# Two transformer blocks on one core: the last pair of maxima in its own slot, outputs in their own list, three things placed elsewhere

## The chip, the core and the metric

The kernel runs on one core of a Trainium2 chip. The core has a matrix engine (TensorE, PE in the profile, with its weight loads as PEld), a vector engine (DVE), a scalar engine (ACT), GpSimd (POOL), and SyncE (SP), which issues most of the DMAs. Each engine works through its own instruction stream in order and waits on semaphores for the others. PE writes only to PSUM, eight banks of 128 x 512 f32, from where DVE or ACT must take the result before the bank is used again. The metric is the device time of one execution in microseconds.

## What is computed

Two layers, each of them self-attention, cross-attention over a context, and a gated feed-forward, on x of 4 x 512 x 320 with a context of 4 x 1601 x 192, 20 heads of 16, all f32:

```python
h1 = _ln(x, n1_g, n1_b)
x = _attn(h1, h1, q1, k1, v1, o1_w, o1_b, heads) + x
h2 = _ln(x, n2_g, n2_b)
x = _attn(h2, context, q2, k2, v2, o2_w, o2_b, heads) + x
h3 = _ln(x, n3_g, n3_b)
a, g = jnp.split(h3 @ ff_w1 + ff_b1, 2, axis=-1)
return a * jax.nn.gelu(g, approximate=False) @ ff_w2 + ff_b2 + x
```

`_attn` is softmax attention: scores of queries and keys, less their row maximum, exponentials, times the values, divided by the sum of the exponentials, and an output projection.

## The kernel before

**Units.** The work of attention is cut into units: one batch row and one group of four heads. A layer has 20 self units (4 rows x 5 groups, 512 keys, 4 chunks of 128 keys), 20 cross units (1601 keys, 13 chunks) and 4 feed-forward units. Numbered over the whole program, layer 0 has self units 0 to 19, cross units 20 to 39 and feed-forward units 40 to 43; layer 1 the same from 44 on.

**Two passes over the scores.** A unit's scores are computed twice. First with queries on partitions, in tiles of 128 queries, only to take the row maxima: PE line L1088 (and L1113 for the 65 last keys of cross units) into tile `sps`, DVE line L1099 (L1123) takes the maximum. `max_end` (L1162 on) then negates and splits the maxima, transposes them on DVE (L1175) and sends them with four small DMAs (L1183) into a tile of rows, `nrows`. The second pass has keys on partitions, in `main`: three accumulating matmuls for each chunk and head (L1336, tile `st`), the third of them adding the negated maxima; ACT takes the exponential (L1346); PE multiplies by the values (L1362, tile `av`), ACT copies that out (L1376 for a unit's first chunk, into the unit's tile `o`, of which there are two; L1381 for the others) and POOL adds it up (L1382).

**Rounds and slots.** The array works with 32 rows per head, so matmuls of four heads run beside one another. A step of `main` handles one chunk: two half-steps, called rounds by the clock of the schedule. In each of them two heads' second-pass scores (three passes of the array) share the array with one *pair* of maximum tiles on the other two row groups (two passes). A self unit has 8 pairs in two lists of 4, a cross unit 26 pairs in two lists of 13; `u.pairs[0]` is served at even rounds and `u.pairs[1]` at odd ones. A unit has as many rounds as pairs: 8 or 26. `giver(u)` (L1643) returns `give(h)`, which hands out the regular pair of round h, always for a unit that comes later: the next unit while it has pairs in the list of that parity, otherwise the one after. It also decides on *extra rounds* (`round_of` on two pairs, one of each list, alone on PE): when the pairs that are due outnumber the rounds left, and when the next unit has any pair left at the last round before its `max_end`, that is round 3 of a self unit and round 21 of a cross unit (the test `rest == 1`).

**The planner.** All other work is put into lists, `chains`, each entry with a cost, a due round and two conditions. At every step `steps` takes the head with the earliest due round, as long as credit allows; entries of cost zero are DMAs and the like. Within a list the order is fixed. Three things here belong to it:

- `add_finish` (L1194) puts what follows a unit's last chunk into the list "divide": first `turn`, which sends the tile `o` to DRAM (`oway`, L1203), two rounds or more after the last chunk. For the last group of a batch row follow the reciprocal of the sums, its way to DRAM and back, and the division of the gathered outputs by parts (`read`, `load`, `divide`, `end`), with waits of several rounds between them.
- `add_turned` (L751) turns batch row b's context: seven pieces, each transposed on DVE (L767) into one of two tiles by turns (`room["turned"]`, in the profile a part of `stages`), and saved to DRAM by a DMA (L775, `ctxT<-stages`). For row 0 of layer 0 this lies under self units 5 to 8; the pieces have due rounds `gap` apart, the last one `gap` before round 70. The transpose of piece i+2 overwrites the tile that the save of piece i reads. `add_context` loads the saved context for the keys (L789).
- `expect` is the planner's model of when PE, ACT and DVE will be done; `bank` (L410) gives out the PSUM bank that this model expects to be free first. It only chooses banks.

**The start.** Before the first unit, the projections and maxima of unit 0 are done by hand, with DMAs on both SP and ACT (`start["on"]`). `at_once(units[2])` issues unit 2's moves: keys on SP, and queries (`q<-halves`, L888) on ACT.

Of the kernel before, what the change touches and what calls it, by code (L numbers as in the profile page):

```python
# [78 lines left out]
def kernel(ctx: ExitStack, tc: tile.TileContext, x, context, ws, out):  # L79
# [313 lines left out]

    chains = {n: deque() for n in ("divide", "project", "norm", "scale", "context", "early", "proj", "values")}
    clock = {"round": 0, "credit": 0.0, "lights": 0, "tiles": None, "ff": False, "cross": False}
    ALIKE = ("project", "early", "proj", "values")
    LIGHT = 0.01
# [42 lines left out]
    def add(chain, cost, f, due, ready=yes, soon=yes):  # L442
        chains[chain].append((cost if isinstance(cost, tuple) else (cost,), due, ready, soon, f))
# [396 lines left out]
    def add_proj(u):  # L840
# [35 lines left out]
        def move(of, pairs, may, gap=0):  # L876

            def f():
                pending[of] -= 1
                if of == "k":  # L880
                    room["sent"] = clock["round"]
                u.moving[of] = clock["round"]
                for to, src in pairs():
                    queue = nc.sync
                    if start["on"]:
                        queue = (nc.sync, nc.scalar)[room["first"] % 2]
                        room["first"] += 1
                    queue.dma_start(out=to.bitcast(F32), in_=src)  # L888
                u.open -= 1
                if not u.open:  # L890
                    u.when = -9 if start["on"] else clock["round"]

            pending[of] += 1
            u.moves[of].append((f, may, gap))
            u.moving[of] = clock["round"]
            if (u.i, of, u) not in movers:
                movers.append((u.i, of, u))
# [266 lines left out]
    def max_end(u):  # L1164

        top, high, low = (u.nm[:, :, i, :] for i in range(3))
        nc.vector.tensor_reduce(
            high.bitcast(F32R), top.rearrange("p j (t o) -> p j t o", o=1), AX.X, ALU.max, negate=True
        )
        nc.vector.tensor_reduce(  # L1170
            low, u.nm[:, :, 0:2, :].rearrange("p j e t -> p j t e"), AX.X, ALU.add, negate=True
        )
        turned = two.tile([P, SLOT], F32, tag="turned", name="turned")

        nc.vector.transpose(turned.rearrange("p (j c) -> p j c", j=HG), u.nm[:, :, 1:3, :].rearrange("p j e t -> p j (e t)"))  # L1175
        busy("dve", 0.6)
        slots = u.rows.bitcast(F32).rearrange("(g s) n -> s g n", s=DH)[0].rearrange("g (t r) -> g t r", t=NQ)

        def rows():
            for i in range(P // SLOT):  # L1180
                part = slice(i * SLOT, (i + 1) * SLOT)
                queue = nc.scalar if start["on"] and i % 2 else nc.sync
                queue.dma_start(out=slots[:, :, part], in_=turned[part, :])  # L1183

        if u.cross and u.before.cross:
            u.rows_of = rows
            errands.appendleft((clock["round"] + 1, yes, rows))
        else:
            rows()

    def add_finish(u):

        when = [clock["round"]]

        def since(i, n):
            return lambda: len(when) > i and clock["round"] >= when[i] + n

        def turn():  # L1200

            way = o_way[u.b % 2]
            dma(out=way[:, u.g * HG : (u.g + 1) * HG].rearrange("s j n -> j s n"), in_=u.o)  # L1203
            if u.g == G - 1:
                held["written"] += 1
                errands.append((clock["round"] + 3, yes, sums))

        def sums():

            den = two.tile([P, N], F32, tag="rT", name="den")[:, : H * N // P]  # L1210
            dma(out=den, in_=o_way[u.b % 2][DH].rearrange("h n -> (h n)").rearrange("(p c) -> p c", p=P))
            when.append(clock["round"])

            def invert():
                nc.vector.reciprocal(den, den)
                busy("dve", 0.75)
                when.append(clock["round"])

            def save():
                dma(out=r_way[u.b % 2].rearrange("h n -> (h n)").rearrange("(p c) -> p c", p=P), in_=den)  # L1220
                errands.append((clock["round"] + 3, lambda: held["open"] < 1, read))

            add("divide", LIGHT, invert, r - 20, yes, since(1, 3))
            add("divide", 0.0, save, r - 20, yes, since(2, 1))

        def read():

            held["read"] += 1
            held["open"] += 1
            aT = one.tile([P, 3, N], F32, tag="aT", name="aT")  # L1230
            way, part = o_way[u.b % 2], {}

            def load(k, at, n):
                heads = slice(at // DH, (at + n) // DH)
                part[k] = two.tile([P, N], F32, tag="rT", name="rT")
                dma(out=aT[:n, k, :], in_=way[:DH, heads])
                dma(
                    out=part[k][:n],
                    in_=r_way[u.b % 2][heads].rearrange("(o j) n -> o j n", o=1).to_broadcast([DH, n // DH, N]),
                )  # L1240
                when.append(clock["round"])

            def divide(k, n):
                nc.gpsimd.tensor_tensor(aT[:n, k, :], aT[:n, k, :], part[k][:n], ALU.mult)  # L1244

            for k, at, n in DK[:2]:
                load(k, at, n)
            first, second, third = DK
            add("divide", 0.0, lambda: divide(0, first[2]), r - 20, yes, since(4, 3))
            add("divide", 0.0, lambda: divide(1, second[2]), r - 20)  # L1250
            add("divide", 0.0, lambda: load(*third), r - 20, yes, since(4, 5 if u.l and not u.cross else 7))
            add("divide", 0.0, lambda: divide(2, third[2]), r - 20, yes, since(5, 3))
            add("divide", 0.0, lambda: end(aT), r - 20)

        def project(aT, t, part):
            cols = slice(part * D // 2, (part + 1) * D // 2)
            ps = bank("ops")
            written(0.93, ps)
            busy("dve", 0.3, ps)
            for k, at, n in DK:  # L1260
                for f, m in tiles_of(P):
                    nc.tensor.matmul(  # L1262
                        ps[f : f + m, : D // 2],
                        lhsT=aT[:n, k, f * NQ + t * SLOT : f * NQ + t * SLOT + m],
                        rhs=wo[:n, k, cols],
                        start=(k == 0),
                        stop=(k == 2),
                    )
            nc.vector.tensor_tensor(xs[u.b][:, t, cols], ps[:, : D // 2], xs[u.b][:, t, cols], ALU.add)

        def end(aT):
            now = clock["round"]
            for t in range(NQ):
                for part in range(2):
                    add(
                        "project", (0.317,) * 3, lambda t=t, part=part: project(aT, t, part),
                        now + 2 + u.nch * t + u.nch // 2 * part, yes, lambda: clock["round"] >= now + 1,
                    )
            add("project", 0.0, done, now + 2 + u.nch * NQ)

        def done():
            held["open"] -= 1
            after(u)

        r = when[0]
        add("divide", 0.0, turn, r - 20, lambda: u.g or held["written"] < held["read"] + 2, since(0, 2))


    late = []
# [283 lines left out]
    def before(u):  # L1573
# [17 lines left out]
        if u.kind == "cross" and u.m == B * G - 2:  # L1591
            loads.extend(load_first(u.l, (4, 2)))
        if u.kind == "self" and u.m == EARLY - 1 and u.l == 0:
            add_turned(0, units[u.i + 1].start + 22, 2)
        if u.kind == "self" and u.m == EARLY:

            add_context(0, lambda s: units[u.i - u.m + B * G].own.update(kv=s["cT"]), u.start + 36, yes)
# [37 lines left out]
    def giver(u):  # L1635
# [15 lines left out]
        def give(h, alone=False):  # L1651
# [7 lines left out]
            for v in coming:  # L1659
                if v not in ahead:  # L1660
                    total += v.steps
                    continue
                total += left(v)


                rest = v.start - (7 if alone else 4) - clock["round"]
                if rest > 0:
                    most = max(most, (total - rest * (not alone)) / (2 * rest))
                if left(v) and (rest == 1 or alone and rest < 1):
                    urgent = urgent or v  # L1670
                    owed = max(owed, 1.0 if alone and rest > -4 else (left(v) + 1) // 2)
            owed += most * went if total else 0.0
# [54 lines left out]
        run("norm")  # L1727
    max_reduce(first)
    max_end(first)
    at_once(units[2])  # L1730
    second = units[1]
    second.pairs = max_pairs(second)
    round_of(second.pairs[0].popleft()[1] + second.pairs[1].popleft()[1])
    add_proj(units[3])
    run("proj")
    run("proj")
    loads.extend(load_x(2))
    for fs in (load_out(0, "o1_w"), load_x(3), load_cross(0)):
        loads.extend(fs)
# [51 lines left out]
```

## Time and profile before

| | us |
|---|---|
| median of 3 runs | 2895.8 (2895.5 to 2897.63) |
| the profiled execution | 2899.26 |
| its span, from the first to the last instruction | 2897.2 |
| PE busy | 2848.3 (98%) |
| DVE, ACT, POOL busy | 1972.1, 1948.9, 1307.5 |

The granted clock of PE was 0.997 over the span. Attention of layer 0 takes about the first 1190 us: its self units up to about 378 us, its cross units after that; then comes the feed-forward, and layer 1 from about 1490 us. A row of the timeline shows the start, the duration, engine and line, operation, tiles (out<-in), the shapes, how many instructions were merged, and in brackets the engine's idle time before them and what ended it.

### The profile page before, as it was taken

What the parts mean: (1) busy time and instruction counts of PE and PEld (TensorE: products, weight loads), DVE (VectorE), ACT (ScalarE), POOL (GpSimd) and SP (SyncE); (2) the same over time, 40 slices, a digit from 0 to 9 for tenths busy, and PEclk for the clock granted to TensorE, in tenths of its full rate; (3) what the DMA queues carried; (4) which work ended last, traced back from release to release, by engine and by line L of the source; (5) the groups of instructions that cost most, each with busy time, mean ns of one, the idle gap of its engine ahead of it and who ended that gap; (6) DMA issues with size and microseconds to landing.
All of it is one profiled execution on the core that took longest, in us unless ns stands there. A gap on an engine that the chain in (4) does not pass through costs nothing.

```text
span 2897.2 us, 83291 instructions
## 1 busy us (share of the span) xinstructions
PE 2848.3 (98%) x35028; PEld 1543.2 (53%) x35028; DVE 1972.1 (68%) x3734; ACT 1948.9 (67%) x4033; POOL 1307.5 (45%) x1420
## 2 busy tenths in 40 slices
PE   9999999999999999999999999999999999999999
PEld 5455555555555555355554555555555555544554
DVE  7867888788888888323257678888878878862221
ACT  4867678888888888501138776788888888893000
POOL 5556345555545546211225653455565564551100
PEclk9999999999999999999999999999999999999999
DMA  4444233232232112200123432221221122122000
GB/s 115 118 111 110 66 82 88 57 93 59 57 87 70 48 50 63 85 18 16 38 52 88 106 91 66 71 69 44 54 73 47 44 72 61 45 72 61 23 22 12
DMA packets 163502, 188.59 MB, mean 65 GB/s; under 512 B 62004, under 2 KB 109112, under 8 KB 163128
## 3 DMA queue, kind: packets, MB, share of 16 engines
q1 hardware_dynamic: 161464, 180.38, 24.5%
q8 instruction: 275, 4.51, 0.6%
q10 hardware_dynamic: 1664, 2.89, 0.4%
q14 instruction: 99, 0.81, 0.1%
HBM read 55.76 MB, written 29.36 MB: 29 GB/s over the span
## 4 chain that ended last, share of the span: by engine, by line
PE 87%; DVE 6%; POOL 3%; DMA 2%; issue 1%; ACT 1%; SPq 0%; POOLq 0%; ACTq 0%; DVEq 0%
PE av L1362 22%; PE st L1336 20%; PE fps L1447 10%; PE sps L1088 8%; PE yps L1554 6%; PE vps L1047 5%; PE ops L1262 4%; PE kps L984 3%; DVE nmax L1099 3%; PE qkps L920 3%; PE fps L1507 3%; PE qps L959 2%; DVE pm L1099 2%; PE sps L1113 1%; POOL hturned L630 1%
## 5 line engine op out<-in xcount | busy, mean ns | idle before, releaser
L1346 ACT ACTIVATE pr<-st 128x512 f32<-128x512 f32 (+1 forms) x2720 | 1404.8, 604 | 309.8 <-PE st L1336 278.2
L1099 DVE TENSOR_REDUCE pm<-sps 128x1 f32<-128x512 f32 (+1 forms) x1920 | 1149.1, 661 | 235.1 <-PE sps L1088 230.2
L1382 POOL TENSOR_TENSOR o<-o,vo 128x512 f32<-128x512 f32 x576 | 739.7, 1284 | 916.6 <-ACT vo L1381 899.0
L1088 PE MATMUL sps<-kT,q 32*128 32x512 f32 (+1 forms) x4800 | 858.2, 419 | 3.8 <-ACT halves L936 1.4
L1336 PE MATMUL st<-q,kT 32*128 32x512 f32 (+1 forms) x5120 | 785.3, 419 | 2.7 <-ACT o L1376 2.1
L1362 PE MATMUL av<-pr,vals 128*32 128x512 f32 (+1 forms) x5440 | 735.1, 606 | 30.9 <-ACT pr L1346 5.6
L1336 PEld LDWEIGHTS st<-q,kT 32*128 32x128 f32 (+1 forms) x5120 | 447.6, 180 | 284.1 <-issue 113.4
L1336 PE MATMUL st<-nrows,ones 32*128 32x512 f32 (+1 forms) x2720 | 560.5, 398 | 0.9 <-DMA nrows<-turned 0.7
L1099 DVE TENSOR_REDUCE nmax<-sps 128x1 f32<-128x512 f32 x640 | 397.0, 683 | 115.2 <-PE sps L1088 113.1
L1088 PEld LDWEIGHTS sps<-kT,q 32*128 32x128 f32 x4800 | 429.9, 183 | 54.7 <-ACT pr L1346 11.2
L1381 ACT COPY vo<-av 128x512 f32<-128x512 f32 x576 | 354.0, 615 | 17.4 <-PE av L1362 10.4
L1518 ACT ACTIVATE gl<-fps,b 128x512 f32<-128x512 f32 x80 | 54.7, 687 | 408.9 <-PE fps L1507 299.1
L1447 PE MATMUL fps<-hT,w 128*128 128x512 f32 x640 | 283.1, 597 | 0.0
L1362 PEld LDWEIGHTS av<-pr,vals 128*32 128x32 f32 (+1 forms) x5440 | 111.1, 108 | 304.2 <-DVE pm L1099 186.7
L1336 PEld LDWEIGHTS st<-nrows,ones 32*128 32x128 f32 (+1 forms) x2720 | 262.9, 180 | 10.1 <-issue 2.0
L1519 DVE SCALAR_TENSOR_TENSOR hid<-fps,b,gl 128x512 f32<-128x512 f32 x80 | 59.7, 748 | 249.2 <-ACT gl L1518 247.1
L1447 PEld LDWEIGHTS fps<-hT,w 128*128 128x128 f32 x640 | 119.3, 190 | 155.0 <-issue 151.6
L1554 PE MATMUL yps<-w,hid 128*128 128x320 f32 x640 | 175.7, 435 | 0.0
L1554 PEld LDWEIGHTS yps<-w,hid 128*128 128x128 f32 x640 | 120.6, 190 | 56.2 <-ACT gl L1518 5.3
L1262 PEld LDWEIGHTS ops<-wo,aT 112*32 112x32 f32 (+1 forms) x3072 | 98.9, 110 | 66.0 <-issue 34.9
L1262 PE MATMUL ops<-wo,aT 112*32 112x160 f32 (+1 forms) x3072 | 125.7, 301 | 2.6 <-POOL aT L1244 2.6
L1123 DVE TENSOR_REDUCE pm<-sps 128x4 f32<-128x508 f32 x160 | 99.0, 682 | 39.8 <-PE sps L1113 38.8
(89 smaller groups left out, 2458.2 us busy)
## 6 DMA issues: line engine op xcount, KB each, us to landing
kT<-stages SPq DMA_DIRECT2D x80, 400.5 KB
oway<-o SPq DMA_DIRECT2D x80, 256.0 KB
q<-halves SPq DMA_DIRECT2D x80, 256.0 KB
q<-halves SPq DMA_DIRECT2D x27, 512.0 KB
kT<-halves SPq DMA_DIRECT2D x40, 256.0 KB
aT<-oway SPq DMA_DIRECT2D x32, 224.0 KB
rT<-rway SPq DMA_DIRECT2D x32, 224.0 KB
hT<-hturned SPq DMA_DIRECT2D x96, 64.0 KB
```

What stands on the lines that cost most here:

```text
L1047: nc.tensor.matmul(ps[f : f + m, :w], lhsT=u.kvT[:n, k, at + f : at + f + m], rhs=wv[:n, k, h0 * DH : h1 * DH], start=(k == 0), stop=(k == ...
L1088: nc.tensor.matmul(own[0][:, :w], lhsT=u.queries(slice(j * SLOT, (j + 1) * SLOT), e, t), rhs=u.kT[j * SLOT : (j + 1) * SLOT, u.k0 + at : u ...
L1099: nc.vector.tensor_reduce(to, own[0][:, :w], AX.X, ALU.max)
L1123: nc.vector.tensor_reduce(u.pm[:, :, j, ns - 1], ps[:, : NQ * w].rearrange("p (t w) -> p t w", w=w)[:, :, :n], AX.X, ALU.max,)
L1262: nc.tensor.matmul(ps[f : f + m, : D // 2], lhsT=aT[:n, k, f * NQ + t * SLOT : f * NQ + t * SLOT + m], rhs=wo[:n, k, cols], start=(k == 0) ...
L1336: nc.tensor.matmul(own[0][:r, :], lhsT=ones[rows, :r] if e == 2 else u.keys(rows, c), rhs=u.rows[rows, :] if e == 2 else u.queries(rows, e ...
L1346: nc.scalar.activation(p[:r], own[0][:r], AF.Exp)
L1362: nc.tensor.matmul(ps[j * SLOT : (j + 1) * SLOT, :], lhsT=columns_of[:r, head : head + SLOT], rhs=pr.pop((c, j))[:r, :], start=True, stop= ...
L1381: nc.scalar.copy(vo, ps)
L1382: nc.gpsimd.tensor_tensor(u.o, u.o, vo, ALU.add)
L1447: nc.tensor.matmul(ps, lhsT=w1[:, k, i * FF + c * P : i * FF + (c + 1) * P], rhs=natural(u.hT[:, k]), start=start, stop=stop,)
L1554: nc.tensor.matmul(ps[:, :D], lhsT=hid[c][:, t * P : (t + 1) * P], rhs=w2[:, c, :], start=(c == 0), stop=(c == NHC - 1),)
```

## The change

```diff
-    chains = {n: deque() for n in ("divide", "project", ...
+    chains = {n: deque() for n in ("way", "divide", "project", ...
...
                     queue.dma_start(out=to.bitcast(F32), in_=src)
+                    if queue is nc.scalar:
+                        expect["act"] += 0.6
...
                 queue = nc.scalar if start["on"] and i % 2 else nc.sync
                 queue.dma_start(out=slots[:, :, part], in_=turned[part, :])
+                if queue is nc.scalar:
+                    expect["act"] = max(expect["act"], expect["dve"]) + 1.05
...
-        add("divide", 0.0, turn, r - 20, lambda: ..., since(0, 2))
+        add("way", 0.0, turn, r - 20, lambda: ..., since(0, 2))
...
-            add_turned(0, units[u.i + 1].start + 22, 2)
+            add_turned(0, units[u.i + 1].start + 22, 3)
...
-                if left(v) and (rest == 1 or alone and rest < 1):
+                if left(v) > bool(not alone and v.pairs[h % 2]) and (rest == 1 or alone and rest < 1):
...
     max_reduce(first)
     max_end(first)
-    at_once(units[2])
     second = units[1]
     second.pairs = max_pairs(second)
     round_of(second.pairs[0].popleft()[1] + second.pairs[1].popleft()[1])
     add_proj(units[3])
     run("proj")
     run("proj")
+    at_once(units[2])
```

- **The last pair.** Where one pair is left at the last round before `max_end`, and it stands in the list that this round serves, no extra round is asked for; the pair goes into its regular slot.
- **Outputs.** `turn` has a list of its own, "way", and is no longer queued behind the divisions of the batch row before.
- **The context pieces** of row 0 are due three rounds apart instead of two, counted back from the same round 70.
- **Unit 2's moves** at the start are issued after the second unit's first round of maxima and after unit 3's projection.
- **The model** `expect["act"]` counts the DMAs that ACT issues at the start. That adds no instruction.

More of the change, by code (lines that the diff above doesn't have):

```diff
@@ L388 @@
         ]
-    chains = {n: deque() for n in ("divide", "project", "norm", "scale", "context", "early", "proj", "values")}
+    chains = {n: deque() for n in ("way", "divide", "project", "norm", "scale", "context", "early", "proj", "values")}
     clock = {"round": 0, "credit": 0.0, "lights": 0, "tiles": None, "ff": False, "cross": False}
@@ L1285, in add_finish @@
         r = when[0]
-        add("divide", 0.0, turn, r - 20, lambda: u.g or held["written"] < held["read"] + 2, since(0, 2))
+        add("way", 0.0, turn, r - 20, lambda: u.g or held["written"] < held["read"] + 2, since(0, 2))
     late = []
```

## The prediction

> **What bounds the kernel now.** I read the page first, then the list of waits of PE alone, then the timeline at each place that the change touches, and the chain of waits there.
>
> ```profile
> span 2897.2 us, 83291 instructions
> ...
> PE 2848.3 (98%) x35028; PEld 1543.2 (53%) x35028; DVE 1972.1 (68%) x3734; ACT 1948.9 (67%) x4033; POOL 1307.5 (45%) x1420
> ...
> PE 87%; DVE 6%; POOL 3%; DMA 2%; issue 1%; ACT 1%; SPq 0%; POOLq 0%; ACTq 0%; DVEq 0%
> ```
>
> PE is the bound: busy for 98% of the span, and 87% of the chain that ended last. So an edit is worth the PE instructions that it saves, or the PE waits that it ends. The waits are few (engine, line, what it waited for: us in total, times, longest):
>
> ```profile
> PE av L1362 <- ACT pr L1346: 5.6, 25, 0.3
> PE av L1362 <- DVE nmax L1099: 5.0, 6, 2.4
> PE av L1362 <- DVE pm L1099: 4.5, 6, 1.3
> ...
> PE st L1336 <- ACT o L1376: 2.1, 1, 2.1
> PE sps L1088 <- ACT halves L936: 1.8, 2, 1.4
> ```
>
> Three single waits stand out: 2.4, 2.1 and 1.4 us. Each lies where one edit works.
>
> **The last pair.** An extra round fires when a unit has a pair left at the last round before its maxima end. Pairs and rounds are equal in number (8 and 8, 26 and 26), so once the rounds run without a lead, the last pair always meets that test. Counted from the loop's rule, it fires where a lead is first lost: in units 0 and 44 (the round then serves the unit after next, and gives a lead of two pairs that lasts through the stage, so that the test stays quiet), in 19 and 63 (a lone pair of short tiles), and in 20 and 64 (again a round for the unit after next). Six rounds go.
>
> Not all of their work does: the pairs remain. In layer 0, units 1 to 20 still owe 6 + 18 x 8 + 26 = 176 pairs when unit 0 begins, and have 156 regular rounds up to the last one. That needs 20 pairs in extra rounds: ten full ones, where now there are ten full ones and the lone one. So unit 0's round comes back, under units 14 to 19, which are made to run ahead for the first cross unit; the lone one goes. In the cross stage the lead of two pairs ends with two empty slots in the last unit but one; without the lead these are filled.
>
> ```profile
> 48.53 0.96 PE L1088 MATMUL sps<-kT,q 32*128 32x512 f32 x9
> 49.10 0.41 PE L1336 MATMUL st<-q,kT 32*128 32x512 f32 x2
> ...
> 324.66 0.76 PE L1088 MATMUL sps<-kT,q 32*128 32x512 f32 x8
> ...
> 325.35 1.18 PE L1047 MATMUL vps<-wv,hT 128*32 128x192 f32 x24
> ...
> 364.00 0.88 PE L1113 MATMUL sps<-kT,q 32*128 32x128 f32 x12
> 364.63 0.50 PE L1336 MATMUL st<-kT 32*128 32x512 f32 x1
> ...
> 409.58 0.39 PE L1336 MATMUL st<-nrows,ones 32*128 32x512 f32 x1
> ...
> 410.00 1.33 PE L1088 MATMUL sps<-kT,q 32*128 32x450 f32 x8
> 411.25 1.07 PE L1362 MATMUL av<-pr,vals 128*32 128x512 f32 x8
> ...
> 1149.23 1.06 PE L1362 MATMUL av<-pr,vals 128*32 128x512 f32 x8
> ...
> 1152.17 1.06 PE L1362 MATMUL av<-pr,vals 128*32 128x512 f32 x8
> ...
> 1154.07 1.06 PE L1362 MATMUL av<-pr,vals 128*32 128x512 f32 x8
> ```
>
> From start to start: unit 0's round costs 49.10 - 48.53 = 0.57, and one under units 14 to 19 costs 325.35 - 324.66 = 0.69, so moving it loses 0.12. The lone round costs 364.63 - 364.00 = 0.63. In unit 20 the round stands ahead of the value matmuls: 411.25 - 410.00 = 1.25. The slots it fills at the stage's end are not free: with pairs a step takes 1152.17 - 1149.23 = 2.94, without them 1154.07 - 1152.17 = 1.90, so 1.04 is paid and 0.21 is left. A layer gains 0.63 + 0.21 - 0.12 = 0.72, both **1.4 us**. Bounds: nothing (PE would have waited for ACT or DVE in these places anyhow) to 3.8 (lone and cross rounds in full, the slots free: 2 x (0.63 + 1.25)). I take 1.4, as each part has its row.
>
> Without the lead a unit's first maximum tiles come two rounds later, at round 4 instead of 2 of the unit two before; that asks for its queries and keys later, not earlier. `max_end` stays behind the same number of reductions in DVE's order, so `nrows` is sent no later.
>
> **The start.** ACT's order changes: the issue of unit 2's queries goes behind the two copies of unit 3's projection.
>
> ```profile
> 36.04 0.60 ACTq L888 DMA_DIRECT2D q<-halves  x1
> 36.77 0.84 ACT L936 ACTIVATE halves<-qkps,scales 128x256 f32<-128x256 f32 x2 [4.13 <-POOL x L623]
> ...
> 35.42 0.50 PE L1336 MATMUL st<-q,kT 32*128 32x512 f32 x2
> 37.29 0.50 PE L1088 MATMUL sps<-kT,q 32*128 32x512 f32 x2 [1.37 <-ACT halves L936]
> ```
>
> PE's first unit waits 1.37 us for those copies, since its bank held the projection. Without the issue ahead of them they start 36.77 - 36.04 = 0.73 earlier. The corrected model of ACT can also give PE another bank, and then the whole 1.37 goes. Bounds 0.73 and 1.37; I take **1.0**, between them. What the copies pass, the queries of unit 2, is first read four rounds into unit 0; behind the later issue stand only that unit's exponentials, whose scores PE has yet to compute. SP issues the same DMAs in the same order.
>
> The Trainium skill (DMA: Bandwidth & Descriptors, "Issuing engines are not separate DMA queues") says that all issuers share 16 DMA engines and that spreading issues over them saves only the sequencer's time. By it alone this edit is worth the 0.73 of issue and no transfer; the row agrees as far as it goes, and the sum would be 0.3 less.
>
> **The context pieces.**
>
> ```profile
> 163.51 7.03 DMA ctxT<-stages
> ...
> 164.15 0.63 DVE L767 STREAM_TRANSPOSE stages<-stages 128x192 f32<-128x192 f32 x2
> ...
> 170.66 0.38 DVE L767 STREAM_TRANSPOSE stages<-stages 128x192 f32<-128x192 f32 x1 [3.25 <-DMA ctxT<-stages]
> ...
> 172.19 1.94 PE L1362 MATMUL av<-pr,vals 128*32 128x512 f32 x8 [2.44 <-DVE nmax L1099]
> ```
>
> The last pieces are squeezed together: the seventh transpose must wait until the save of the fifth, issued at 163.51, has landed 7.03 later. DVE stands 3.25 us, the maxima behind it are late, their banks stay taken, and PE waits 2.44. With due rounds 49, 52, ... 67 instead of 56, 58, ... 68 the fifth piece goes out two to six rounds sooner; two rounds are a step, 2.5 us or more (rows under the slower rival), so that its save lands near 168 or before, about when DVE asks for it, 170.66 - 3.25 = 167.4. Same work on DVE, the same 14 DMAs on SP, only earlier, so the wait goes: **2.4**. Bounds: -0.8 (another piece meets its save: 3.25 on DVE again instead of 2.44 on PE) to 2.4.
>
> **The outputs.**
>
> ```profile
> 243.68 0.62 ACT L1376 COPY o<-av 128x512 f32<-128x512 f32 x1
> 258.64 0.61 ACT L1376 COPY o<-av 128x512 f32<-128x512 f32 x1
> 275.23 0.58 ACT L1376 COPY o<-av 128x512 f32<-128x512 f32 x1 [4.68 <-DMA oway<-o]
> ...
> 264.90 10.26 DMA oway<-o
> ...
> 275.87 0.73 PE L1336 MATMUL st<-q,kT 32*128 32x512 f32 x3 [2.08 <-ACT o L1376]
> ```
>
> These copies begin units 12, 13 and 14. There are two `o` tiles, so unit 14 must wait until unit 12's tile, filled from 243.68 on, is in DRAM. Its `turn` was queued behind the division of the row before, went out at 264.90, six rounds after it could have, and took 10.26. ACT stood 4.68, PE 2.08. In a list of its own it goes out with the step of the copy at 258.64, near 259, and lands near 269, before ACT asks at 275.23 - 4.68 = 270.6. Gain **2.1**. The same queue delays units 7, 17, 51, 56 and 61 by two to six rounds; there PE shows no such wait, so nothing is counted. Ahead of it on SP the turn passes the four `nrows` DMAs and the queries' moves: 0.6 us each time, and `nrows` has a whole step to spare. Bounds 0 to 2.1.
>
> **The sum.** 1.4 + 1.0 + 2.4 + 2.1 = 6.9 us. The profiled execution took 2899.26, of which 2897.2 span; after the change span 2890.3 and 2892.4 in all. The median of the runs shown is 2895.8, 3.5 below that execution, so the forecast on its scale is 2895.8 - 6.9 = **2888.9**. A measurement of this kernel tells 0.2%, 5.8 us, from no change: 2890.0 is the border, 1.1 above the forecast.
>
> **Rivals.**
>
> *The waits only move* (2894.4). The saves, turns and `nrows` share SP and the DMAs; brought forward they meet others, and the 2.4 and 2.1 reappear in another step. For it: a 256 KB turn took 10.26 us. What the start wins is lost to them too, and only the 1.4 of the last pair stays. The Trainium skill (DMA: Bandwidth & Descriptors, the same section) would have it so: moved transfers interleave with whatever else is in flight. Against it: both waits came from a late issue, seen in the rows.
>
> *The saving is not one* (2890.3). The rule that spreads extra rounds over time asks for them all again. Then 1.4 is lost. Against it: the count of 176 and 156.
>
> *More waits go* (2885.4). DVE's two kinds of wait hold 5.0 + 4.5 = 9.5 us, 2.4 of it counted; half of the remaining 7.1, mostly in the same early stage, goes too as steps there are less crowded: 3.5 more.
>
> *Slower* (2908.9). The altered model and order shift the choice of PSUM banks for the whole program, and PE meets banks that are not yet read.
>
> ```profile
> 263.97 1.06 PE L1362 MATMUL av<-pr,vals 128*32 128x512 f32 x8
> ...
> 266.50 1.06 PE L1362 MATMUL av<-pr,vals 128*32 128x512 f32 x8
> ...
> 269.22 1.06 PE L1362 MATMUL av<-pr,vals 128*32 128x512 f32 x8
> ```
>
> Steps of the same work take 2.53 and 2.72: 0.19 for where a tile lands. There are about 650 steps. If one in six (105) goes from the short to the long form, 20 us are lost; from 67 steps (6.9 + 5.8 = 12.7 us) it counts as slower. Against it: the model takes the latest of its engines at every tile, so that a shift of 2 us at the start dies out, and banks are alike.
>
> **Chances.** Forecast 0.43 (0.28 of it below 2890.0), waits move 0.22, no saving 0.07 (0.02 below), more go 0.18, slower 0.10. Faster by over 0.2%: 0.28 + 0.02 + 0.18 = 0.48; within: 0.15 + 0.22 + 0.05 = 0.42; slower 0.10. Range: from the forecast with the upper bounds (3.8 + 1.37 + 2.4 + 2.1 = 9.7) and the 3.5 on top, 2882.6, to the moved waits with the context's lower bound and no saving (2895.8 + 0.8, and 2 us of spread, as the runs shown have between 2895.5 and 2897.63), 2898.6. About 0.15 is left out, most of it the slower case.
>
> **What would show it.** The wait of PE for `o` and DVE's wait for `ctxT<-stages` are gone from the lists; PE's wait for `halves` is 0.7 or less; no round of eight `sps` stands ahead of `av` near 410, and no lone short round near 364. It is wrong if new single waits over 1 us stand between 120 and 300 us, or if the cross stages change by more than a microsecond.

## The result, and the profile after

| | before | after |
|---|---|---|
| median, us (14 runs of each) | 2895.2 (2892.41 to 2897.63) | 2889.67 (2888.57 to 2891.47) |
| ratio, 95% interval | | 0.9982 [0.9975, 0.9989] |
| the profiled execution | 2899.26 | 2890.09 |
| its span | 2897.2 | 2888.3 |

The change wins 5.5 us, 0.2%. The forecast was 6.9 us and 2888.9. The total came out near, but partly by luck: the last pair won far more than its term, the context pieces lost where they should have won, and the two errors nearly cancel.

The head of the page of after:

```profile
span 2888.3 us, 83210 instructions
...
PE 2836.0 (98%) x35028; PEld 1538.6 (53%) x35028; DVE 1975.4 (68%) x3734; ACT 1948.9 (67%) x4033; POOL 1307.6 (45%) x1420
```

PE runs the same 35028 matmuls in 12.3 us less of busy time: the pairs of the removed rounds now run beside other matmuls, and, as shown below, the clock was higher. Idle time grew by 3.4. The list of PE's waits in after (engine, line, releaser: us in total, times, longest):

```profile
PE st L1340 <- DMA nrows<-turned: 9.8, 7, 6.8
...
PE av L1366 <- DVE nmax L1101: 2.2, 4, 0.8
...
PE sps L1090 <- ACT halves L938: 0.2, 1, 0.2
```

The three single waits of before (2.44 for DVE, 2.08 for `o`, 1.37 for `halves`) are gone. A new one of 6.8 us, for the rows of negated maxima, is longer than the three together. (Line numbers are 2 higher than before from L888 on, and 4 higher behind L1185.)

**Where it comes from.** PE's timeline in after, where it stands longest:

```profile
177.69 0.80 PE L1340 MATMUL st<-nrows,ones 32*128 32x512 f32 x2 [6.77 <-DMA nrows<-turned]
```

On DVE, the source of these rows had been ready at 163.59 + 0.21 = 163.80:

```profile
163.59 0.21 DVE L1177 STREAM_TRANSPOSE turned<-nmax 128x32 f32<-128x32 f32 x1
```

SP's timeline in after shows what it did in the ten microseconds between:

```profile
164.64 0.59 SPq L1207 DMA_DIRECT2D oway<-o  x1
165.32 0.55 SPq L775 DMA_DIRECT2D ctxT<-stages  x1
171.12 2.49 SPq L789 DMA_DIRECT2D w<-ctxT  x4
173.72 2.67 SPq L1185 DMA_DIRECT2D nrows<-turned  x4
```

And the list of waits of SP's own queue, from 155 to 180 us:

```profile
SPq L789 <- DMA ctxT<-stages: 5.2, 1, 5.2
SPq L1207 <- POOL o L1386: 3.8, 1, 3.8
```

SP issues in order. Unit 7's `turn` (L1207), now six rounds earlier, stood 3.8 us until POOL had added up its tile:

```profile
163.33 1.28 POOL L1386 TENSOR_TENSOR o<-o,vo 128x512 f32<-128x512 f32 x1
```

It ends at 164.61, and the issue follows at 164.64. The context's save went out behind it at 165.32. Next in the program stood the load of the context (L789), which reads what that save writes, and waited 5.2 us for it to land. `nrows` stood behind the load. The chain of waits of after has the landings:

```profile
165.32 5.78 DMA ctxT<-stages
...
175.79 1.65 DMA nrows<-turned
```

165.32 + 5.78 = 171.10, and the load goes out at 171.12; 175.79 + 1.65 = 177.44, and PE starts at 177.69.

**Where the rest went.** The first copies of units into `o` (ACT, L1376 before, L1380 after) are landmarks: every unit has one. In after:

```profile
43.42 0.62 ACT L1380 COPY o<-av 128x512 f32<-128x512 f32 x1
59.81 0.62 ACT L1380 COPY o<-av 128x512 f32<-128x512 f32 x1
162.78 0.62 ACT L1380 COPY o<-av 128x512 f32<-128x512 f32 x1
187.57 0.62 ACT L1380 COPY o<-av 128x512 f32<-128x512 f32 x1
257.40 0.61 ACT L1380 COPY o<-av 128x512 f32<-128x512 f32 x1
269.15 0.62 ACT L1380 COPY o<-av 128x512 f32<-128x512 f32 x1
```

And in before, where they are not shown yet:

```profile
45.43 0.62 ACT L1376 COPY o<-av 128x512 f32<-128x512 f32 x1
64.43 0.62 ACT L1376 COPY o<-av 128x512 f32<-128x512 f32 x1
167.07 0.62 ACT L1376 COPY o<-av 128x512 f32<-128x512 f32 x1
187.68 0.62 ACT L1376 COPY o<-av 128x512 f32<-128x512 f32 x1
```

They are units 0, 1, 8, 9, and in after also 13 and 14. After less before: -2.0 at unit 0 (the start), -4.6 at unit 1 (the extra round of unit 0: 2.6), -4.3 at unit 8, -0.1 at unit 9 (`nrows`: 4.2 lost), -1.2 at unit 13, -6.1 at unit 14, -5.9 at unit 15 (289.69 and 295.55). Two of these are far larger than the waits that went. Between units 13 and 14 it is 4.8 for a PE wait of 2.08: unit 14's copy is itself the instruction that ACT held up for 4.68 in before, and PE had other work for the rest of that time. At unit 15 the gain since unit 13 is 4.6; by then before has also had a stretch of low clock that after has not. At the start it is 2.0 for a wait of 1.37; there the granted clock has most of the reason.

**The clock after a wait.** Windows of before where the clock was low (start and end, length, PE busy and its instructions, granted clock, DMA share, GB/s):

```profile
40.00:44.00 4.00, 3.95 (x54) 0.69 1.00 253
...
172.00:176.00 4.00, 3.81 (x32) 0.57 0.16 27
...
276.00:280.00 4.00, 4.00 (x45) 0.75 0.23 69
...
336.00:340.00 4.00, 4.00 (x37) 0.57 0.19 49
...
1488.00:1492.00 4.00, 3.79 (x27) 0.72 0.28 58
```

The same view of after:

```profile
176.00:180.00 4.00, 2.31 (x16) 0.50 0.49 123
...
276.00:280.00 4.00, 3.92 (x67) 1.00 0.09 22
...
1484.00:1488.00 4.00, 4.00 (x33) 0.61 0.72 186
```

In windows of half a microsecond the clock is 1.00 or 0.50, and it is 0.50 for about 3.4 us at a time, or for two or three times that (in after for 10.24 us from 173.02 on, around the wait for `nrows`). Three of before's five dips begin within 3 us of the end of one of its three single waits; a dip of 3.41 us then costs half of that, 1.71 us of PE work, on top of the wait. PE's timeline shows the same 48 projections behind the wait for `halves` in before:

```profile
38.77 3.81 PE L1047 MATMUL vps<-wv,hT 128*32 128x192 f32 x48
```

and at the same place in after:

```profile
38.41 2.16 PE L1049 MATMUL vps<-wv,hT 128*32 128x192 f32 x48
```

That is 1.65 us for identical work. The prediction priced waits and never looked at the clock behind them.

The Trainium skill (TensorE: Matmul & The Clock Gate, "What's actually happening") has the clock drop to half after an idle window of about 3.4 us, and says that the windows run freely. The half rate and the 3.4 us agree with these rows. So do the free windows: before's five dips begin at 39.09, 172.21, 278.02, 336.05 and 1489.75 us, which are 39, 31, 17 and 338 times 3.413 us apart. The idle time needed does not: here the clock fell after waits of 1.37, 2.08 and 2.44 us.

Summed over each profiled execution, (1 - granted clock) x PE busy time of half-microsecond windows:

| kernel | span | lost to low clock | span less that | against before |
|---|---|---|---|---|
| before | 2897.2 | 8.5 (5 dips) | 2888.7 | |
| after | 2888.3 | 4.5 (2, one long) | 2883.8 | -4.9 |
| e1_pair | 2890.4 | 6.8 (4) | 2883.6 | -5.1 |
| e2_way | 2891.6 | 6.7 (4) | 2884.9 | -3.8 |
| e3_gap | 2895.6 | 8.5 (4, one long) | 2887.1 | -1.6 |
| e4_start | 2891.1 | 5.1 (2, one long) | 2886.0 | -2.7 |
| e5_later | 2885.6 | 5.1 (2, one long) | 2880.5 | -8.2 |
| e6_gap2 | 2883.2 | 1.7 (1) | 2881.5 | -7.2 |
| e7_thin | 2893.1 | 6.8 (3, one long) | 2886.3 | -2.4 |
| e8_model | 2886.9 | 0 | 2886.9 | -1.8 |
| e9_gapway | 2895.4 | 8.0 (3, two long) | 2887.4 | -1.3 |
| e10_selfpair | 2891.6 | 6.8 (3, one long) | 2884.8 | -3.9 |
| e11_move | 2891.4 | 5.1 (3) | 2886.3 | -2.4 |

So of the 8.9 us between the two profiled spans 4.0 are clock, and before's profiled execution, 4 us above its median, had five dips where other kernels had none to four. The dips differ from execution to execution, so a single look at one kernel is uncertain by several times 1.7 us; the medians below decide. The repeats agree: of the 33 runs of before beside the first four experiments, the five with a mean clock of 0.999 took 2892.8 us on average, the five with 0.996 took 2898.9.

### The profile page after: what moved, and what is told of

It reads as the page before. It is cut to its first block, busy times and chain, and to the rows that moved or that the text cites. A ratio compares the mean times of both kernels' runs of the same rounds, so it can differ in the third digit from the quotient of the medians.

```text
span 2888.3 us, 83210 instructions
## 1 busy us (share of the span) xinstructions
PE 2836.0 (98%) x35028; PEld 1538.6 (53%) x35028; DVE 1975.4 (68%) x3734; ACT 1948.9 (67%) x4033; POOL 1307.6 (45%) x1420
## 4 chain that ended last, share of the span: by engine, by line
PE 86%; DVE 9%; POOL 2%; DMA 1%; issue 1%; ACT 1%; SPq 1%; ACTq 0%; POOLq 0%; DVEq 0%
PE av L1366 22%; PE st L1340 19%; PE fps L1451 10%; PE sps L1090 8%; PE yps L1558 6%; PE vps L1049 5%; PE ops L1266 4%; DVE nmax L1101 3%; PE kps L986 3%; PE qkps L922 3%; PE fps L1511 3%; DVE pm L1101 2%; PE qps L961 2%; DVE pm L1125 2%; PE sps L1115 1%
```

## The experiments

The four parts alone, each against runs of the kernel before on the same chip (median 2894.94, five rounds).

**The last pair alone**

```diff
-                if left(v) and (rest == 1 or alone and rest < 1):
+                if left(v) > bool(not alone and v.pairs[h % 2]) and (rest == 1 or alone and rest < 1):
```

> The kernel before with the changed test for the last pair alone. Theory A (from the two traces side by side): each removed full round was worth more than its matmuls, about 2.5 us in units 0 and 44 and 1.2 to 1.6 us in units 20 and 64, the lone rounds 0.7 us each; less what comes back under units 14 to 19 and in the filled slots, 6 to 8 us below before. Theory B (the price in the prediction, by the matmuls alone): 1.4 us below before. Both expect the same count of PE matmuls, and no round of eight sps ahead of av in the first cross unit.

Measured: 2890.41, ratio 0.9986 [0.9978, 0.9995]: 4.5 us, three times the 1.4 forecast, though short of the 6 to 8 of the first theory. From one landmark to the next, in us (e10_selfpair, which keeps the rounds of the cross units, comes below):

| from the first copy of | before | e1_pair | e10_selfpair |
|---|---|---|---|
| unit 0 to unit 1 (round removed) | 19.00 | 16.38 | 16.38 |
| unit 16 to 17 (round comes back) | 13.83 | 15.37 | 15.38 |
| unit 19 to 20 (lone round removed) | 15.70 | 14.90 | 14.93 |
| unit 20 to 21 (round removed) | 47.12 | 45.53 | 47.11 |
| unit 21 to unit 44 | 1068.29 | 1071.09 | 1068.48 |
| unit 44 to 45 (round removed) | 15.76 | 13.23 | 14.62, with a dip |
| unit 60 to 61 (round comes back) | 14.01 | 15.56 | 15.57 |
| unit 63 to 64 (lone round removed) | 16.77 | 15.41 | 15.42 |
| unit 64 to 65 (round removed) | 46.34 | 45.14 | 46.33 |
| unit 65 to the end | 1037.62 | 1038.34 | 1037.64 |

So 2.6 is won at unit 0, 1.6 at unit 20, 2.5 at unit 44 and 1.2 at unit 64. The round that comes back costs 1.5 under unit 16 and under unit 60, where DVE takes 24 maxima for 20. The lone rounds were worth 0.8 each: before's 16.77 is high, since six other profiles that keep the lone round have 16.21 to 16.23 from unit 63 to 64. The cross stage of layer 0, with the feed-forward behind it, gives 2.8 back, that of layer 1 0.7. The copies of units 16 and 17 in before and, with L1380, in after:

```profile
311.04 0.62 ACT L1376 COPY o<-av 128x512 f32<-128x512 f32 x1
324.87 0.62 ACT L1376 COPY o<-av 128x512 f32<-128x512 f32 x1
...
305.20 0.62 ACT L1380 COPY o<-av 128x512 f32<-128x512 f32 x1
320.58 0.62 ACT L1380 COPY o<-av 128x512 f32<-128x512 f32 x1
```

**The outputs' own list alone**

```diff
-    chains = {n: deque() for n in ("divide", ...
+    chains = {n: deque() for n in ("way", "divide", ...
-        add("divide", 0.0, turn, r - 20, ...
+        add("way", 0.0, turn, r - 20, ...
```

> The kernel before with the outputs in a list of their own, alone. Theory A: PE's wait for o (2.08 us in the profile of before) goes, and with it the copies and exponentials that were late behind ACT's 4.68 us: about 4.8 us below before, all between the first copy of unit 13 and that of unit 14. Theory B (the prediction): 2.1 us. Theory C (moved transfers only interleave with others): 0, with a new wait of PE for nrows.

Measured: 2893.27, ratio 0.9993 [0.9984, 1.0001]: 1.7 us by the medians, not clear of zero. PE's wait for `o` is gone from the list, and so is the dip near 278. From unit 13's copy to unit 14's the profile wins the 4.8 us of Theory A, but the medians stand nearer to the 2.1 of Theory B. The sign of Theory C is there too, a new wait of PE of 1.04 us for `nrows` at 176.13. In the profiles of the kernels that keep the old list, the wait for `o` was 2.08 (before), 2.2 (e1_pair), 1.8 (e3_gap), 1.6 (e7_thin), 1.9 (e10_selfpair), 1.2 (e11_move), 0.6 (e8_model) and 0.5 us (e4_start): the start edit alone takes most of it away, so these two parts don't simply add up.

**The context pieces alone**

```diff
-            add_turned(0, units[u.i + 1].start + 22, 2)
+            add_turned(0, units[u.i + 1].start + 22, 3)
```

> The kernel before with the context pieces three rounds apart, alone. Theory A: DVE's wait for the save of a piece goes (2.4 us of PE), but the load of the saved context is now issued on SP ahead of unit 9's nrows, SP waits for the last save, and PE waits about 7 us for nrows near 175 us: 4 us slower than before. Theory B (the prediction): 2.4 us faster, no such wait.

Measured: 2895.13, ratio 1.0003 [0.9995, 1.0012]: nothing. Both theories missed. From the list of PE's waits in this kernel, and from PE's timeline in this kernel and then in before:

```profile
PE av L1362 <- DVE nmax L1099: 2.2, 4, 0.8
...
182.06 2.76 PE L1262 MATMUL ops<-wo,aT 96*32 96x160 f32 x56 [3.31 <-POOL aT L1244]
...
182.71 2.12 PE L1262 MATMUL ops<-wo,aT 96*32 96x160 f32 x56 [0.64 <-POOL aT L1244]
```

DVE's longest is 0.8 instead of 2.4, as forecast, and no long wait for `nrows` came. PE was earlier at the next thing that it needs, the gathered outputs, which POOL multiplies by the reciprocals (`aT`), and waited 3.31 there instead of 0.64. In before the two waits are 2.44 + 0.64 = 3.08. Five other profiles with the old gap (e1_pair, e4_start, e8_model, e10_selfpair, e11_move) divide the same sum otherwise: 1.25 to 1.44 for DVE and 1.74 to 1.86 for `aT`, 3.1 to 3.2 together; e7_thin has 2.44 and 0.33. So whatever DVE's wait gives up, POOL's takes.

**The start alone** (the model's lines and the move)

```diff
+                    if queue is nc.scalar:
+                        expect["act"] += 0.6
...
+                if queue is nc.scalar:
+                    expect["act"] = max(expect["act"], expect["dve"]) + 1.05
...
-    at_once(units[2])
     second = units[1]
...
+    at_once(units[2])
```

> The kernel before with unit 2's moves issued later and the model of ACT's issues, alone. Theory A: 2.0 us below before, all of it before unit 0's first copy of o (45.4 us in the profile of before). Theory B (the prediction): 1.0 us, 0.73 to 1.37.

Measured: 2892.69, ratio 0.9989 [0.998, 0.9998]: 2.2 us by the medians. In the pair of profiles unit 0's copy is 2.0 us earlier, as Theory A has it; how much of that is clock comes below.

Alone the four win 4.5 + 1.7 - 0.2 + 2.2 = 8.2 us; together 5.5. The long wait for `nrows` stands only in the sum, so the next question was which parts make it. Two kernels take it away from the changed kernel; the median of before beside them was 2893.94.

**The context's load three rounds later**, so that it stands behind the next `nrows`

```diff
-            add_context(0, lambda s: ..., u.start + 36, yes)
+            add_context(0, lambda s: ..., u.start + 39, yes)
```

> The changed kernel with the load of the saved context due three rounds later (u.start + 39 for 36), so that it goes out on SP behind unit 9's nrows instead of ahead of them. Theory A: the 6.8 us wait of PE for nrows near 177 us is that order on SP and nothing else; it goes, and the time is 5 to 7 us below the changed kernel, about 2884 (0.39% below before). Theory B: SP and the DMAs are crowded there whatever the order, and the wait moves to the output projection or the next unit's copies: 2 us or less below the changed kernel.

Measured: 2885.15, ratio 0.9969 [0.9956, 0.9981], against 0.9982 for the changed kernel; 0.0013 is 3.8 us, though the two intervals overlap and 3.8 lies between the two theories. SP's timeline has `nrows` right behind the save and ahead of the load:

```profile
165.67 0.54 SPq L775 DMA_DIRECT2D ctxT<-stages  x1
166.31 3.46 SPq L1185 DMA_DIRECT2D nrows<-turned  x4
171.58 5.63 SPq L789 DMA_DIRECT2D w<-ctxT  x8
```

PE's timeline has 1.20 us where 6.77 stood:

```profile
172.43 0.50 PE L1340 MATMUL st<-nrows,ones 32*128 32x512 f32 x2 [1.20 <-DMA nrows<-turned]
```

The load still waits for its save (1.7 us), but nothing urgent is behind it. A part of Theory B holds too: at 177.10 PE now waits 2.16 us for POOL's `aT`. By its median this kernel is the fastest of all here.

**The changed kernel with the old gap of 2**

```diff
-            add_turned(0, units[u.i + 1].start + 22, 3)
+            add_turned(0, units[u.i + 1].start + 22, 2)
```

> The changed kernel with the context pieces two rounds apart again. Theory A: together with the earlier turn the wider gap costs 4 us (2.4 won on DVE's wait, 6.8 lost on nrows), so this is 3 to 5 us below the changed kernel, with PE's wait of about 2.4 us for DVE back near 165 us and none for nrows. Theory B: the gap is worth in company what it is alone, 0.2 us, and this equals the changed kernel.

Measured: 2886.25, ratio 0.9973 [0.9962, 0.9984]; the longest wait for `nrows` is 1.0, and DVE's is back at 1.4. It wins 7.7, near the 4.5 + 1.7 + 2.2 = 8.4 of the three other parts alone. In this company the wider gap costs 2.6 us by the ratios, a little less than Theory A's 3 to 5; the intervals overlap, so the next kernel looks at the wait itself.

**Gap and outputs' list alone**, on the kernel before, with both edits shown above

> The kernel before with the wider gap and the outputs' own list together, and nothing else. Theory A: the long wait for nrows needs two things ahead of it in SP's order, the turn of unit 7, which waits for POOL's last addition, and the load of the context, which waits for the last save; the gap alone showed no such wait, the two together show one of 2 us or more near 175 to 183 us. Theory B: the wait needs PE to be 4 us ahead (the last pair, the start), and the two together show none.

Measured: 2897.23, a single run. PE's list:

```profile
PE st L1336 <- DMA nrows<-turned: 7.2, 2, 6.8
```

SP's own list has the same two waits ahead of it, 3.8 us for POOL's addition and 5.2 us for the save. All three are those of after to a tenth, without the other parts: the wait is made by these two edits together, and by neither alone.

**What the last pair is worth, and why**

Unit 0's extra round, with its four DVE maxima over 64 of the 512 keys, and unit 44's likewise, on the kernel before:

```diff
-            own = []
+            own, thin = [], room.get("thin")
...
-                nc.vector.tensor_reduce(to, own[0][:, :w], AX.X, ALU.max)
+                nc.vector.tensor_reduce(to, own[0][:, : 64 if thin else w], AX.X, ALU.max)
...
+                if u.i in (0, 44) and h == 3:
...
```

> The kernel before, extra rounds kept, but the four maxima of the extra round in units 0 and 44 are taken over 64 of the 512 keys, which takes most of their time off DVE and leaves every matmul. (The row maximum only shifts the exponent, so any of a row's scores serves.) Theory A: those rounds cost their DVE time, 4 x 0.6 us in a stretch where DVE is never idle: this wins about 2 us in each, 4 us together, in the steps right after them. Theory B: they cost their matmuls on PE (0.57 us each): this wins nothing.

Measured: 2892.33, ratio 0.9992 [0.9983, 1.0001]: 1.6 us by the medians, not clear of zero, so the landmarks have to tell. From unit 0's copy to unit 1's it takes 61.87 - 44.25 = 17.62 us, against 64.43 - 45.43 = 19.00 before and 61.84 - 45.46 = 16.38 with the round gone altogether (e1_pair): the thin reductions give 1.4 of the 2.6 with PE's work unchanged. Around unit 44 it is 14.51 against 15.76 before and 13.23 after: 1.25 of 2.5. No dip of the clock lies between these copies. DVE's timeline in before shows the price:

```profile
49.29 2.49 DVE L1099 TENSOR_REDUCE nmax<-sps 128x1 f32<-128x512 f32 x4 [1.00 <-PE sps L1088]
51.69 0.16 DVE L1167 TENSOR_REDUCE nmax<-nmax 128x16 fp32r<-128x16 f32 x1
```

and in this kernel:

```profile
48.12 0.62 DVE L1099 TENSOR_REDUCE nmax<-sps 128x1 f32<-128x64 f32 x4 [1.01 <-PE sps L1088]
```

The extra four maxima take 2.49 us and stand ahead of `max_end` of the unit that PE needs next; `max_end` begins at 51.69 here. In after, where they are gone, it begins 5.4 us earlier, 2.0 of them from the start:

```profile
46.32 0.17 DVE L1169 TENSOR_REDUCE nmax<-nmax 128x16 fp32r<-128x16 f32 x1
```

The 1.2 that are left are about the 0.62 of thin maxima and the 0.57 of matmuls added up: an estimate, not a test.

The test for the last pair in self units alone:

```diff
-                if left(v) and (rest == 1 or alone and rest < 1):
+                if left(v) > bool(not alone and not u.cross and v.pairs[h % 2]) and (rest == 1 or alone and rest < 1):
```

> The kernel before with the changed test for the last pair in self units only; cross units keep their extra round and its lead of two pairs. Theory A (from the traces): the cross part wins 1.6 us at units 20 and 64, pays 0.6 us for the filled slots, and loses up to 2 us on the way through the stage, so it is worth nothing: this equals the pair edit alone within 1 us. Theory B: the cross part is worth its 1.2 us of matmuls a layer: this is 2 us slower than the pair edit alone.

Measured: 2891.29, ratio 0.9986 [0.9976, 0.9995] beside a median of 2895.51, the ratio of e1_pair. Its cross stages hardly drift (0.2 from unit 21 to unit 44 in the table); those of e1_pair lose 2.8. So the rounds saved at units 20 and 64 are paid back during the cross stages, where the lead of two pairs was worth something. A part of the price is a wait that before and e10_selfpair don't have in layer 0's cross stage: without the lead PE waits for `nrows` there, 1.3 us in two waits in e1_pair and 0.8 in after. The longer one in e1_pair:

```profile
788.94 0.50 PE L1336 MATMUL st<-nrows,ones 32*128 32x512 f32 x2 [0.86 <-DMA nrows<-turned]
```

The rest is spread over many units, mostly at 0.1 to 0.2 us each, and its cause is open.

**What the start is worth**

Only the model's lines:

> The kernel before with the model of ACT's issues alone (no instruction moved). Theory A: the start's gain is the choice of the bank, so PE's wait for halves (1.4 us) goes here too, and from the first projection to the first value matmul it takes about 29.2 us instead of 31.3. Theory B: it is the issue taken from ahead of ACT's copies; here the wait of 1.4 us stays and the stretch takes 31.3 us.

Measured: 2888.97, a single run. PE's timeline shows no wait for `halves`, though ACT's copies were no earlier than before:

```profile
35.44 0.49 PE L1340 MATMUL st<-q,kT 32*128 32x512 f32 x2
...
37.18 0.49 PE L1340 MATMUL st<-nrows,ones 32*128 32x512 f32 x2 [1.00 <-DMA nrows<-turned]
```

Another bank removes the whole 1.37; a wait of 1.00 for unit 0's own `nrows` is next, after eight matmuls instead of two. This execution has no dip at all.

Only the move:

> The kernel before with unit 2's moves issued later, the model of ACT unchanged. Theory A (the model's choice of bank did it all): from the first projection to the first value matmul 30.5 us or more, PE's wait for halves still over 0.6 us. Theory B (the issue ahead of the copies did it): under 29.5 us and no such wait.

Measured: 2893.46, a single run. PE's timeline:

```profile
37.06 0.50 PE L1088 MATMUL sps<-kT,q 32*128 32x512 f32 x2 [0.69 <-ACT halves L936]
```

The wait is halved, 1.37 to 0.69, where 0.73 less was forecast.

The stretch from the first of the 48 `qkps` matmuls ahead of these rows (32.69 in before) to unit 0's copy of `o` (45.43) puts the two together. It is 12.74 in before, 12.62 to 12.79 in e1_pair, e3_gap and e10_selfpair, with a dip in it each time; 11.16 and 11.11 in e7_thin and e9_gapway, with the same wait for `halves` but no dip; 10.64 in e11_move, and 10.39 to 10.41 in all five kernels with the model's lines. So the start edit takes 0.7 us where there is no dip (11.1 to 10.4), and 1.6 more in executions whose clock would have dropped there. (e2_way stands apart: its clock dropped earlier, at 30 us, its wait was 0.54 and the stretch 10.31.)

## Why the prediction was right, and where it was not

**What bounds the kernel.** Right, PE; but the argument that an edit is worth the instructions saved or the waits ended left out the rate at which PE runs. The windows of before would have told it: the two waits that were priced at 2.4 and 2.1 stand beside windows of 0.57 and 0.75 of the clock. A wait of that kind costs its length and 1.7 more when the clock falls.

**The last pair: mechanism and count right, size wrong.** Six rounds go, the lone ones among them, which were worth 0.8 each for the 0.63 forecast. At unit 20 there is no extra round of eight `sps` ahead of `av` any more:

```profile
402.78 0.39 PE L1340 MATMUL st<-nrows,ones 32*128 32x512 f32 x1
402.88 0.27 PE L1115 MATMUL sps<-kT,q 32*128 32x128 f32 x2
403.19 1.07 PE L1366 MATMUL av<-pr,vals 128*32 128x512 f32 x8
```

403.19 - 402.78 = 0.41 from the last `st` to `av`, where 411.25 - 409.58 = 1.67 stood: 1.26, as forecast. The mis-sized term is the round of units 0 and 44, priced at the 0.57 us that PE's matmuls took from start to start. It measured 2.6 and 2.5, and half of that is DVE's four reductions. The round that comes back was priced the same way, at 0.69, and measured 1.5. So moving it was taken to lose 0.12 and wins about 1.0 in each layer; with the lone rounds that is 1.0 + 0.8 a layer, 3.6 for both, where e10_selfpair measured 4.2. The sentence behind the low price is "`max_end` stays behind the same number of reductions in DVE's order, so `nrows` is sent no later". Under unit 0 `max_end` stands behind four reductions fewer, and in the cross stage PE waits for `nrows` as it did not before. The cross part fails the other way: it was forecast to leave 0.21 a layer, and it is worth nothing. With both, 1.4 became 4.5, above the upper bound of 3.8.

**The start: right about the wait, not about what it is worth.** The move shortens the wait by 0.68 of the 0.73 forecast, and the model's bank removes the whole 1.37. But a wait of 1.00 for `nrows`, which the prediction doesn't have, stands right behind it, so that the stretch is only 0.7 shorter where there is no dip, about the lower bound. That 1.0 became 2.2 by the medians fits the clock, which fell behind the wait for `halves` in four of the six profiled executions that had it at 1.37 us or more, and at that place in none of the six with one of the start edits: 0.7 and four sixths of 1.65 are 1.8, an estimate. The Trainium skill's rule on issuers (DMA: Bandwidth & Descriptors, "Issuing engines are not separate DMA queues") would have had no more than the issue; the move alone agrees, with 0.68, and the bank choice goes past it.

**The context pieces: wrong, in the step "the wait goes".** DVE's wait went. But alone the win moved to POOL's `aT` (0.64 to 3.31 us), a wait that the prediction doesn't look at, and with the outputs' list the sign turned. For that the sentence that failed is in the outputs' part: "Ahead of it on SP the turn passes the four `nrows` DMAs and the queries' moves: 0.6 us each time, and `nrows` has a whole step to spare." That counts the time of issue. What a DMA costs those behind it on an in-order queue is its issue and its own wait: 3.8 us for POOL, 5.2 us for the save. The load of the context, which the edit doesn't touch, was not in the working at all. Forecast was a gain of 2.4; measured in the profile a loss of 6.77 - 2.44 = 4.3 in waits.

**The outputs: about right.** 1.7 by the medians for 2.1, with an interval that just reaches zero. In the pair of profiles 4.6 are won from unit 13's copy to unit 15's: the wait of 2.08 and the dip behind it of 1.71 are 3.8 of that.

**The rivals.** "The waits only move" named the place, SP, and was half right: alone, the context pieces' wait moved to POOL, and in company one moved to SP. It gave up too much, since the start's and the last pair's gains stayed. "The saving is not one" falls by e1_pair, and "slower, by banks" by every run here. The sign "wrong if new single waits over 1 us stand between 120 and 300 us" is met by the 6.77: this step was wrong. That the total came near is luck: alone, the last pair won 3.1 more than its term and the start 1.2 more, the outputs 0.4 less and the context pieces 2.6 less, and together the four lose another 2.7, which fits the wait for `nrows`: 6.9 + 3.1 + 1.2 - 0.4 - 2.6 - 2.7 = 5.5.

## What to carry to other kernels

Before a DMA is moved in a queue that issues in order, write down what it waits for and what is queued behind it; small transfers that the bounding engine needs go ahead of ones that wait for others' work. Price a saved piece of work on every engine that it loads, at the place where it stands, not only on the one that bounds the kernel. And read the granted clock behind each PE wait: here a wait of 1.2 to 2.4 us often cost 1.7 us more. When a wait goes, look for the next one that ends just behind it: here two of the three gave most of their time to another.

## What the hardware showed

- The matrix engine's clock fell to half for 3.4 us after waits shorter than that: 1.37 to 1.42, 2.08 and 2.44 us. It did not fall after each: the wait for `halves` of 1.37 to 1.42 us was followed by a dip in before, e1_pair, e3_gap and e10_selfpair, and by none in e7_thin and e9_gapway. The wait for `o` was followed by one after 1.2 to 2.1 us in five profiles, and by none after 2.2 in e1_pair. A dip near 1485 us, where layer 1 begins, stands in most kernels with no wait of more than 0.25 us ahead of it; what sets it off there is open.
- A save of a context piece took 7.03 us to land in before and 5.78 in after, a 256 KB turn 10.26, a small `nrows` 1.65.
